# A convolution with group norm on one core: VectorE's and ScalarE's instruction queues aligned to a boundary of 128 instructions

## Chip, cores and metric

One core of a Trainium2 chip. The metric is the device time of one execution in microseconds; a kernel's time is the median of several runs. A profile is a separate record of one execution with every instruction and every DMA packet.

## What is computed

The input x has 8 images of 32 channels, 128 x 128, in float32. Group norm over 16 groups (two channels each) is followed by a 3 x 3 convolution done by FFT in the reference, and the result is added to x:

```
def _gn(v, G=16, eps=1e-5):
    g = v.reshape(B_, G, C_ // G, H_, W_)
    ...
    return ((g - m) / jnp.sqrt(s + eps)).reshape(v.shape)
...
    fout = jnp.einsum('bihw,oihw->bohw', fx, wf)
    sp = jnp.fft.ifft2(fout, norm='ortho').real
    ...
    out = sp[:, :, sh:sh + out_h, sw:sw + out_w]
    return out + bias[None, :, None, None]
...
x = x + _L0_conv_ref(_gn(x), L0_conv_weight, L0_conv_bias, 1, 1)
```

The reference pads to 256 x 256, multiplies the spectra, and cuts out a 128 x 128 window that begins 64 rows and columns in. Only the upper left part of that window holds convolution output; elsewhere the padding gives zero, so there the result is x plus the bias.

## The kernel before

**Layout.** The host splits each image into its four phases (even and odd rows and columns), so that the 32 channels times 4 phases fill 128 partitions, with 64 x 64 values of an image in each. Images lie in SBUF in pairs (`x0` to `x3`) and are updated in place. The weights and the bias come in one small array, `wb_sb`, and ScalarE spreads them into the 128 x 512 tile `w_sb` (line 181).

**Order of the work.** There is no scheduler. Every instruction is emitted through `Queues.__call__` (line 63), which puts it at the end of its engine's queue with the semaphore waits that it needs, so the order of the source is the order on each engine. `sp` issues all transfers: eight loads at the start (line 117, images 0 and 1 in halves, 2 and 3 whole, the rest in pairs, the weights after the first half) and seven stores (line 320: pairs 0 and 1 whole, images 4, 5 and 6 one by one, image 7 in two parts).

For an image, VectorE takes statistics in eight pieces (line 210) and joins them (221); ScalarE forms the terms (223, 226); TensorE averages over the group by the matrix `avg` (234); ScalarE and VectorE alternate over small columns to get scale and shift (243, 248, 252, 254, 257); ScalarE writes the normalised part needed into `g` (266) and adds the bias to the parts of x without convolution output (281). TensorE multiplies in three chunks of four float32 matmuls (297); VectorE adds product and bias to x (312), and the store follows. The statistics of image n + 2 and the normalising of image n + 1 run while TensorE multiplies image n.

**The top of the program.** After a barrier of all engines, GpSimd builds a mask (141 to 151), VectorE writes `eps` (152) and makes `avg` (155 to 163), and ScalarE loads its table and runs one activation on `warm` (166). Then ScalarE waits for the weights and VectorE for the first half of image 0.

**Instruction queues.** [...] The kernel's own part is some 115 instructions on ScalarE, 105 on VectorE and 437 on TensorE. [...]

## Time and profile before

| | before |
|---|---|
| median of 4 runs | 84.71 us (84.43, 84.48, 84.94, 85.06) |
| profiled execution's own time | 84.43 us |
| its span in the profile | 83.2 us |
| first load issued, first data packet | 0.79 us, 1.79 us |
| TensorE's last matmul ends | 73.4 us |
| last store issued | 74.93 us |
| HBM read, written | 16.82 MB, 16.78 MB |

In the lines of the profile, L297 is line 297 of the kernel; PE is TensorE's matmul, PEld its weight load, DVE is VectorE, ACT ScalarE, SPq the queue of SyncE that issues transfers. A row of digits shows the span in 40 equal slices, with the busy share of each in tenths. A line of DMA queues gives packets, MB, and the packets' time as a share of 16 DMA engines. A wait line reads: engine and line that waited, what released it, total us, times, longest us. A line that begins with a stretch such as 42.00:52.00 gives its length, then busy time and count of PE, PEld, DVE, ACT and POOL, the granted TensorE clock, the DMA share and GB/s.

### The profile page before, as it was taken

What the parts mean: (1) busy time and instruction counts of PE and PEld (TensorE: products, weight loads), DVE (VectorE), ACT (ScalarE), POOL (GpSimd) and SP (SyncE); (2) the same over time, 40 slices, a digit from 0 to 9 for tenths busy, and PEclk for the clock granted to TensorE, in tenths of its full rate; (3) what the DMA queues carried; (4) which work ended last, traced back from release to release, by engine and by line L of the source; (5) the groups of instructions that cost most, each with busy time, mean ns of one, the idle gap of its engine ahead of it and who ended that gap; (6) DMA issues with size and microseconds to landing.
All of it is one profiled execution on the core that took longest, in us unless ns stands there. A gap on an engine that the chain in (4) does not pass through costs nothing.

```text
span 83.2 us, 697 instructions
## 1 busy us (share of the span) xinstructions
PE 65.0 (78%) x214; PEld 39.4 (47%) x214; DVE 54.5 (66%) x103; ACT 51.8 (62%) x102; POOL 2.3 (3%) x8
## 2 busy tenths in 40 slices
PE   0000998999999999999999999999999999920000
PEld 0000531666666566656666666666566666600000
DVE  0339927982999799699969969996997250060000
ACT  6019437994995798499569958965994895000000
POOL 6400000000000000000000000000000000000000
PEclk9999999999999999999999999999999999996555
DMA  2899999999997999699989998999899999999991
GB/s 47 339 410 433 418 429 465 402 465 394 504 504 315 441 504 449 299 489 504 260 347 425 473 457 378 425 504 410 378 402 425 441 433 441 418 441 387 428 421 65
DMA packets 2211, 33.63 MB, mean 404 GB/s; under 512 B 256, under 2 KB 288, under 8 KB 416
## 3 DMA queue, kind: packets, MB, share of 16 engines
q1 hardware_dynamic: 2208, 33.60, 96.1%
q8 instruction: 1, 0.02, 0.1%
q14 instruction: 2, 0.02, 0.1%
HBM read 16.82 MB, written 16.78 MB: 404 GB/s over the span
## 4 chain that ended last, share of the span: by engine, by line
PE 76%; DMA 8%; DVE 2%; ACT 2%; SPq 1%; issue 1%
PE ps L297 70%; DMA x<-x_dram 8%; PE ps_w L330 5%; DVE x L312 2%; PE ps_m L234 1%; SPq L117 1%; ACT g L266 1%; ACT std L252 0%; ACT square L243 0%; ACT rstd L257 0%; DVE rstd L254 0%; DVE var L248 0%
## 5 line engine op out<-in xcount | busy, mean ns | idle before, releaser
L297 PE MATMUL ps<-g,w_sb 128*128 128x363 f32 (+1 forms) x192 | 59.0, 464 | 0.2 <-ACT g L266 0.2
L297 PEld LDWEIGHTS ps<-g,w_sb 128*128 128x128 f32 x192 | 35.2, 189 | 21.5 <-ACT g L266 2.0
L210 DVE BATCH_NORM_STATS2 stats<-x 128x6 f32<-128x512 f32 x64 | 38.7, 677 | 2.3 <-DMA x<-x_dram 2.2
L281 ACT ACTIVATE x<-x,bs_sb 128x1984 f32<-128x1984 f32 (+1 forms) x16 | 23.9, 1540 | 0.3
L312 DVE SCALAR_TENSOR_TENSOR x<-ps,bs_sb,x 128x1089 f32<-128x1089 f32 (+2 forms) x9 | 10.5, 1180 | 7.2 <-PE ps L297 7.2
L266 ACT ACTIVATE g<-x,rstd 128x396 f32<-128x396 f32 (+1 forms) x16 | 12.7, 838 | 0.3
L330 PE MATMUL ps_w<-x,avg 128*128 128x512 f32 x6 | 5.8, 1111 | 8.2 <-DMA x<-x_dram 8.2
L330 PEld LDWEIGHTS ps_w<-x,avg 128*128 128x128 f32 x6 | 1.7, 326 | 9.2 <-DMA x<-x_dram 8.2
L243 ACT ACTIVATE square<-ps_m 128x7 f32<-128x7 f32 x8 | 1.4, 176 | 5.7 <-PE ps_m L234 5.7
L223 ACT ACTIVATE terms<-bs_sb,mv 128x8 f32<-128x8 f32 x8 | 2.4, 302 | 3.6 <-DVE mv L221 3.6
L248 DVE COPY var<-ps_m 128x1 f32<-128x1 f32 x8 | 1.3, 158 | 5.1 <-ACT square L243 5.1
L234 PEld LDWEIGHTS ps_m<-terms,avg 128*128 128x128 f32 x16 | 3.2, 205 | 2.8 <-ACT terms L226 1.3
L252 ACT ACTIVATE std<-var 128x1 f32<-128x1 f32 x8 | 2.4, 295 | 1.8 <-DVE var L248 1.8
L257 ACT ACTIVATE rstd<-ps_m,rstd 128x1 f32<-128x1 f32 x8 | 2.1, 261 | 1.8 <-DVE rstd L254 1.8
L254 DVE RECIPROCAL rstd<-std 128x1 f32<-128x1 f32 x8 | 1.3, 164 | 2.9 <-ACT std L252 2.9
L221 DVE BATCH_NORM_AGGREGATE mv<-stats 128x2 f32<-128x48 f32 x8 | 3.0, 372 | 0.3
L181 ACT ACTIVATE bs_sb<-wb_sb 32x9 f32<-32x9 f32 x4 | 0.8, 210 | 3.7 <-DMA wb_sb<-wb_dram 3.6
L181 ACT ACTIVATE w_sb<-wb_sb 32x64 f32<-32x64 f32 (+2 forms) x16 | 2.8, 244 | 0.0
L234 PE MATMUL ps_m<-terms,avg 128*128 128x9 f32 x16 | 2.5, 230 | 0.0
L226 ACT ACTIVATE terms<-mv,eps 128x1 f32<-128x1 f32 x8 | 2.2, 279 | 0.0
L166 ACT ACT_TABLE_LOAD x1 | 1.3, 1283 | 0.8 <-PEq L411 0.8
L243 ACT ACTIVATION_READ_ACCUMULATOR square<-ps_m 128x1 f32 x8 | 1.6, 194 | 0.0
(12 smaller groups left out, 3.6 us busy)
## 6 DMA issues: line engine op xcount, KB each, us to landing
x<-x_dram SPq DMA_DIRECT2D x2, 4096.0 KB, 34.5
out_dram<-x SPq DMA_DIRECT2D x2, 4096.0 KB, 17.1
out_dram<-x SPq DMA_DIRECT2D x3, 2048.0 KB, 10.6
x<-x_dram SPq DMA_DIRECT2D x4, 1024.0 KB, 7.5
x<-x_dram SPq DMA_DIRECT2D x2, 2048.0 KB, 17.1
out_dram<-x SPq DMA_DIRECT2D x1, 1056.0 KB, 8.2
out_dram<-x SPq DMA_DIRECT2D x1, 992.0 KB, 11.8
wb_sb<-wb_dram SPq DMA_DIRECT2D x1, 40.5 KB, 4.6
```

The source lines that it names most:

```text
L181: return put("act", lambda e: e.activation(to, of, AF.Identity), weights_in, w_zero, mark=True)
L210: lambda e: e.bn_stats(stats[img][:, s, :], xts[img][:, STATS * s : STATS * (s + 1), :].rearrange("p h w -> p (h w)"),),
L221: "dve", lambda e: e.bn_aggr(mv, stats[img].rearrange("p n s -> p (n s)")), stats_ok[img], mark=True
L223: put("act", lambda e: e.activation(t[:, 0:NSIGN], signs, AF.Identity, scale=mv[:, 0:1]), mv_ok, bias_ok)
L234: lambda e: e.matmul(ps_ms[:, 0 : NSIGN + 1], avg, terms[img], start=True, stop=True),
L243: lambda e: e.activation(squares[img], ps_ms[:, 1:NSIGN], AF.Square, accum_out=var[:, 0:1]),
L252: "act", lambda e: e.activation(std, var[:, 0:1], AF.Sqrt, bias=var[:, 1:2]), square_ok, copied, mark=True
L266: lambda e: e.activation(g[:, rows, :], xt[:, LO + rows.start : LO + rows.stop, LO:W], AF.Identity, bias=rstd[:, 1:2], scale=rstd[:, 0:1],),
L281: put("act", lambda e: e.activation(part, part, AF.Identity, bias=bias_sb), *free, mark=True)
L297: lambda e: e.matmul(ps[:, 0:rows, 0 : N - dc], w_sb[:, k * P : (k + 1) * P], g[:, top : top + rows, dc:N], start=(k == 0), stop=(k == 3),),
L312: lambda e: e.scalar_tensor_tensor(part, in0=ps, scalar=bias_sb, in1=part, op0=ALU.add, op1=ALU.add),
L330: "pe", lambda e: e.matmul(ps_w, avg, piece, start=True, stop=True),
```

## The change

Behind the opening barrier, ahead of all other work of the kernel, VectorE and ScalarE get one directive each:

```diff
 NSIGN = 8
+PAGE = 128
 LANDED = 16
...
     put = Queues(nc)
+
+    for engine in (nc.vector, nc.scalar):
+        engine.addr_align(PAGE, offset=0, max_nops=0)
```

`addr_align` is not an instruction that computes. The loader reads it when it lays out the engine's final stream and places the next instruction at a multiple of 128 instruction slots[...]; the slots left over ahead of it are dead, and with `max_nops=0` one branch skips them. TensorE, GpSimd and SyncE get none. Nothing else changes: all instructions, waits and transfers are those of before, in the same order on every engine, four lines further down in the source.

## Prediction

> **What bounds the kernel now.** I read the page first: busy shares, the forty slices, the DMA queues, then the chain.

> ```profile
> PE 65.0 (78%) x214; PEld 39.4 (47%) x214; DVE 54.5 (66%) x103; ACT 51.8 (62%) x102; POOL 2.3 (3%) x8
> DMA  2899999999997999699989998999899999999991
> GB/s 47 339 410 433 418 429 465 402 465 394 504 504 315 441 504 449 299 489 504 260 347 425 473 457 378 425 504 410 378 402 425 441 433 441 418 441 387 428 421 65
> q1 hardware_dynamic: 2208, 33.60, 96.1%
> q8 instruction: 1, 0.02, 0.1%
> q14 instruction: 2, 0.02, 0.1%
> ```

> The compute engines are busy 62 to 78%, the data queue 96% of all 16 DMA engines' time. The last slice (81.1 to 83.2 us) holds 65 GB/s: most DMA engines have finished there, a few haven't. Three packets are labelled "instruction"; the change touches those.

> The chain says "PE ps L297 70%", which misleads: it follows releases, not queues. The DMA queue's own waits and a table of stages put this right.

> ```profile
> SPq L376 <- DMA out_dram<-x: 7.9, 1, 7.9
> ...
> 42.00:52.00 10.00, 10.00 (x37) 6.26 (x36) 8.86 (x18) 8.02 (x14) 0.00 (x0) 1.00 1.00 429
> ...
> 72.00:81.00 9.00, 1.39 (x5) 0.59 (x4) 1.48 (x2) 0.00 (x0) 0.00 (x0) 0.70 0.99 422
> 81.00:83.20 2.20, 0.00 (x0) 0.00 (x0) 0.00 (x0) 0.00 (x0) 0.00 (x0) 0.50 0.19 77
> ```

> The end waits 7.9 us for stores. The DMA share is 0.98 to 1.03 from 2 to 81 us, also after TensorE's last matmul (73.4 us). The last store is issued at 74.93 us, but by the packet records no DMA engine reaches its data before 78.4 us: 3.4 MB of older stores stand ahead. So 33.6 MB through 16 DMA engines set the end, and the latest of the 16 ends it.

> The packet records give each engine's finish: the 4-byte semaphore write by which every DMA engine closes each transfer. Microseconds behind the first engine, sorted:

> ```
> load ending 22.1 us: 0 .02 .05 .06 .17 .19 .19 .19 .21 .21 .22 .24 .25 .30 .32 .40
> load ending 42.1 us: 0 .07 .11 .12 .21 .36 .36 .37 .38 .41 .42 .57 .61 1.15 1.48 1.82
> last store, 81.0 us: 0 .07 .11 .12 .36 .36 .37 .38 .41 .43 .57 .61 .89 1.16 1.48 1.82
> ```

> Three engines fall far behind between 22 and 42 us, and since none is ever idle, none catches up. In that stretch lie the three instruction packets:

> ```profile
> DMA packets 29, 0.44 MB, mean 1106 GB/s; under 512 B 14, under 2 KB 14, under 8 KB 14
> q1 hardware_dynamic: 27, 0.43, 259.0%
> q14 instruction: 2, 0.02, 11.9%
> ```

> That is the DMA view of 31.8 to 32.2 us: both q14 packets. The one of q8 lies in 40.4 to 40.6 us. I joined each packet's end to the start next to it (all within 25 ns), which gives 16 unbroken rows from 30 to 46 us:

> - engine A: instruction packet at 31.815 us (8192 bytes, 0.333 us), then a data packet of 1.868 us where its like take 1.213; closes the load at 43.58 (the 1.48 above)
> - engine B: at 32.109 us (8192 bytes, 0.427 us), then a data packet of 1.672; closes at 43.92 (the 1.82)
> - engine C: at 40.486 us (q8, 16384 bytes, 1.016 us); closes at 43.25 (the 1.15)

> The three late engines are the three that carried an instruction packet.

> [...]

> **The change part by part.** Nothing is removed; no instruction of the computation changes its order or queue on any engine. ACT and DVE get one directive each, behind the opening barrier and ahead of their first instruction. The loader turns it into one jump over unused slots.

> 1. *The jump.* [...] From A's 0.333 us and SP's 1.0 us from issue (0.79) to first packet (1.79) I estimate at most 1.4 us. Both are covered:

> ```profile
> ACT bs_sb L181 <- DMA wb_sb<-wb_dram: 3.6, 1, 3.6
> DVE stats L210 <- DMA x<-x_dram: 2.2, 1, 2.2
> DVE avg L155 <- POOL pair L145: 1.7, 1, 1.7
> ```

> ACT may start 3.6 us later before the weight spreading (5.87 us) moves; DVE 1.7 us before its first addition moves and some 3.8 us before the statistics (5.60 us) do. The instructions queued behind the jump (table load, warm-up; eps, the averaging matrix) all lie in that cover. Without it, 1.5 us more are free: the tightest store (image 5, issued at 63.84) is reached by the DMA engines at 66.3 and needs 1.0 to start. SP and POOL get no directive. Cost 0.

> 2. *The two q14 fetches.* I take them to be ACT's and DVE's crossing into their next block: ACT is near its row 60 of 115, DVE near row 50 of 105[...]. After the jump each body begins at a block's first slot. ACT's body is 113 instructions and DVE's 103, both under 128, so neither crosses again before its last instruction. Crossings and their fetches move from 32 us to 0.8 us. The data packets begin at 1.79 us, so a fetch of 0.33 to 0.43 us fits ahead if it starts by 1.35; one that waits the full 1.0 us of SP's start touches the first load.

> 3. *The end.* Without their fetches A and B should close with the other thirteen (0 to 0.89). C keeps its own: 1.157. End gain: 1.821 - 1.157 = 0.664 us. The two packets alone would be worth less; the slowed data packets behind them (0.655 and 0.459) go too.

> Sum against the profiled execution (84.43 us, span 83.2): span 82.5, time 83.77. The median of the four runs is 0.28 above that execution, so 84.71 - 0.66 = 84.05 us. Bounds of this step: no gain if the fetches still meet data at full price; 1.821 - 0.889 = 0.93 us if C gets lighter too (its packet runs amid slow packets on all engines around 41 us, so it may vary).

> **Rivals.**

> *The fetch lands in the first load* (partial). For: 0.8 plus 1.0 is 1.8 us. Against: the first data packets are staggered over 1.79 to 2.45 us anyway. A lag of 0.4 to 0.6 plus 0.33 stays below C, full gain; plus the full 0.99 (0.333 + 0.655) gives 1.4 to 1.6, gain 0.2 to 0.4: 84.4 us.

> *The change doesn't do what it says.* The fetch may not be tied to the block's edge where I think, or what the runtime runs after the body crosses a block (ACT's body ends some 15 slots short of it) and fetches at 70 us under the stores. Then the late engine is only another: 84.6 to 84.8 us.

> *Slower: the jump throws the fetched blocks away.* ACT and DVE each fetch two blocks afresh at the top, under the first load. Two at A's price are 2 x 0.99 = 1.98 us on one DMA engine, never made up: 0.4 to 0.6 plus 1.98 against 1.82 is 0.6 to 0.8 us slower, 85.3 to 85.5. It decides once over 1.2 us is added to one engine (1.82 - 0.61). Against: at 32 us the next block was evidently there, as neither engine stopped.

> *No fetch matters.* DMA bytes are equal and 8 KB is 0.02% of them, which speaks for no change; the table of finishes speaks against it.

> **How the numbers follow.** Fetches clear of the data: 0.58, 84.05 us, own range 83.6 to 84.4. Partial: 0.14, 84.4. No effect: 0.19, 84.7. Slower by refetch: 0.09, 85.4. About 1% (0.85 us) is what a measurement of this kernel can tell from no change. The four runs spread 84.43 to 85.06; if the high ones are a worse day of A or B, the main case gains more than 0.66. So 0.31 of faster by over 1% comes from the main case (half of it), 0.64 within 1%, and 0.05 slower by over 1% from the refetch with a third block. The range 83.5 to 85.0 leaves out the refetch and the far end of the main case.

> **What would show it.** In the changed kernel no q14 packet at 10 to 75 us; two before 2 us; one q8 packet near 40 us still; one late DMA engine (C) instead of three, so the last slice emptier; busy times of all engines as before, TensorE's last matmul at 73.4 within 0.2 us. Wrong if two engines still close 1.4 us or more behind, if q14 packets appear near 70 us, or if ACT's or DVE's first instruction moves by over 3 us.

## The result and the profile after

No change that can be measured: the median is 84.80 us after (84.06 to 86.25) and 84.67 us for the kernel before, run beside it (84.06 to 86.45). The ratio is 1.0011, 95% interval 0.9995 to 1.0027. Forecast was 84.05 us. The profiled execution after took 84.8 us (span 83.6); that of before had taken 84.43. The medians here count all executions, the ratios leave out those over 1.5% above the fastest of the same kernel.

The page after, same rows as before:

```profile
PE 65.0 (78%) x214; PEld 39.4 (47%) x214; DVE 54.6 (65%) x103; ACT 51.8 (62%) x102; POOL 2.3 (3%) x8
DMA  2899999999999899799898999999899999999991
q1 hardware_dynamic: 2208, 33.60, 95.6%
q14 instruction: 2, 0.02, 0.1%
q8 instruction: 1, 0.02, 0.1%
```

The same work, the same full DMA engines, the same three instruction packets. They did move. The DMA view of the kernel after, first for 1.8 to 3.6 us, then its row for 31.8 to 32.2 us, where both q14 packets lay before:

```profile
q1 hardware_dynamic: 63, 0.52, 89.6%
q14 instruction: 2, 0.02, 6.0%
```

```profile
q1 hardware_dynamic: 24, 0.43, 248.5%
```

So the fetches (the instruction packets of q14, called ScalarE's and VectorE's from the runs with one directive alone, below) left the middle and came to the top, but not ahead of the data. By the packet records they start at 1.828 and 3.344 us, and the first data packet at 1.812. They also take longer there: 0.958 and 0.760 us, against 0.333 and 0.427 before.

The timeline at the top of the kernel after (start, duration, engine) shows the jump:

```profile
0.80 0.38 SPq L121 DMA_DIRECT2D x<-x_dram  x1
...
1.23 1.28 ACT L170 ACT_TABLE_LOAD   x1 [1.23 <-PEq L415]
...
1.42 0.06 DVE L156 MEMSET eps<- 128x1 f32 x1 [1.42 <-PEq L415]
```

The table load stands 0.45 us later than before (0.78), `eps` 0.56 us later (0.86). The trace has the jump itself as a branch at 0.786 us on ScalarE (0.033 us) and at 0.818 on VectorE (0.047 us); the rest, 0.41 and 0.55 us, is a stall behind it. Both lie in the cover that the prediction named. ScalarE's wait for the weights is 3.9 us after (3.6 before), so the jump reached nothing.

The first loads themselves end later. TensorE waits for the second half of image 0; after, then before:

```profile
PE ps_w L334 <- DMA x<-x_dram: 9.1, 1, 9.1
```

```profile
PE ps_w L330 <- DMA x<-x_dram: 8.2, 1, 8.2
```

All that hangs on TensorE moves with it: its last matmul ends at 74.3 us (73.4 before) and the last store is issued at 75.86 (74.93). The DMA engines reach that store's data at 78.46 us, as before (78.43), so this doesn't set the end.

How far the 16 DMA engines are behind the first one, from the semaphore writes in the packet records, as in the prediction (us). The first row is the sixth load of x; further down, "the third transfer" is the second half of image 0, which the first engine ends at 7.3 to 7.9 us (9.6 where the loads are held):

```
load ending 22.1 us: 0 .05 .09 .10 .15 .17 .18 .19 .20 .22 .29 .38 .42 1.07 1.26 1.29
load ending 42.1 us: 0 .01 .09 .14 .23 .24 .35 .46 .46 .48 .58 .62 1.44 1.66 2.08 2.17
last store, 81.0 us: 0 .09 .14 .23 .24 .35 .46 .46 .48 .58 .62 .74 1.66 1.84 2.08 2.17
```

Before, all 16 were within 0.40 us at 22 us. Now three are late there already, one more than there are fetches, and the latest ends 2.17 us behind instead of 1.82. Stages show the same tail. Before:

```profile
81.00:82.00 1.00, 0.00 (x0) 0.00 (x0) 0.00 (x0) 0.00 (x0) 0.00 (x0) 0.50 0.35 144
82.00:83.00 1.00, 0.00 (x0) 0.00 (x0) 0.00 (x0) 0.00 (x0) 0.00 (x0) 0.50 0.06 25
```

After:

```profile
81.00:82.00 1.00, 0.00 (x0) 0.00 (x0) 0.00 (x0) 0.00 (x0) 0.00 (x0) 0.50 0.40 169
82.00:83.00 1.00, 0.00 (x0) 0.00 (x0) 0.00 (x0) 0.00 (x0) 0.00 (x0) 0.50 0.20 84
```

The next to last number is the DMA share; one engine alone is 0.06. From 82 us on there is about one engine's work left before, three engines' after.

### The profile page after: what moved, and what is told of

The parts are those of the page before. It is cut to its first block, busy times and chain, and to the rows that moved or that the text cites. A ratio compares the mean times of both kernels' runs of the same rounds, so it can differ in the third digit from the quotient of the medians.

```text
span 83.6 us, 699 instructions
## 1 busy us (share of the span) xinstructions
PE 65.0 (78%) x214; PEld 39.4 (47%) x214; DVE 54.6 (65%) x103; ACT 51.8 (62%) x102; POOL 2.3 (3%) x8
## 3 DMA queue, kind: packets, MB, share of 16 engines
q1 hardware_dynamic: 2208, 33.60, 95.6%
## 4 chain that ended last, share of the span: by engine, by line
PE 76%; DMA 9%; DVE 2%; ACT 2%; SPq 1%; issue 1%
PE ps L301 70%; DMA x<-x_dram 9%; PE ps_w L334 5%; DVE x L316 2%; PE ps_m L238 1%; SPq L121 1%; ACT g L270 1%; ACT std L256 0%; ACT square L247 0%; ACT rstd L261 0%; DVE rstd L258 0%; DVE var L252 0%
## 6 DMA issues: line engine op xcount, KB each, us to landing
wb_sb<-wb_dram SPq DMA_DIRECT2D x1, 40.5 KB, 5.4
```

## Experiments

The theory: a fetch costs the DMA engine that carries it up to 1 us wherever it meets data, no engine catches up, and the latest engine ends the kernel. The rival: the fetches are too small to matter and the late engines have another cause. In every profile here the execution's time is 1.64 to 1.70 us more than the last engine's last semaphore write (84.43 - 82.77 before, 84.80 - 83.15 after, 86.61 - 84.91 in the slowest below). That the latest engine sets the time is thereby given; the question is what makes it late.

**Directives ahead of the barrier** (twice, then with TensorE, for which `(nc.tensor, 2 * PAGE)` is added to the loop). The jumps are put in front of the opening barrier, 0.7 us earlier:

```diff
-    for engine in (nc.vector, nc.scalar):
-        engine.addr_align(PAGE, offset=0, max_nops=0)
+    block = nc.m.functions[0].blocks[0]
+    ahead = list(block.instructions)
+    for engine, page in ((nc.vector, PAGE), (nc.scalar, PAGE)):
+        engine.addr_align(page, offset=0, max_nops=0)
+    every = list(block.instructions)
+    for align in every[len(ahead):]:
+        at = next(n for n, i in enumerate(ahead) if i.engine == align.engine)
+        ahead.insert(at, align)
+    block.instructions = ahead
```

> The two directives stand ahead of the opening barrier instead of behind it, so the jumps come some 0.7 us earlier. Theory (a fetch costs its DMA engine about 1 us wherever it meets data, and the latest of the 16 engines ends the kernel): the q14 packets start at about 1.1 us, 1.04 us after the jump as in the changed kernel, and are over before the first data packet at 1.8 us; only the engine of TensorE's fetch (q8) stays late, the spread of the 16 engines at the end falls from 2.17 us to about 1.2, and the end comes 0.5 to 0.7 us earlier than before (ratio 0.992 to 0.995), less up to 0.2 us by which the barrier may open later. Rival (the lateness of some DMA engines isn't the fetches' doing): the spread stays near 2 us and the ratio is 1.000 or above.

Ratio 0.9986 (0.9963 to 1.0010), medians 84.66 and 84.66 us. The DMA view of 1.1 to 1.9 us, all packets that there are:

```profile
DMA packets 2, 0.02 MB, mean 20 GB/s; under 512 B 0, under 2 KB 0, under 8 KB 0
## 3 DMA queue, kind: packets, MB, share of 16 engines
q14 instruction: 2, 0.02, 5.1%
```

The fetches (1.331 and 1.485 us, 0.324 us each) are clear of the data, which start at 1.953, 0.16 us late. Yet the gain isn't there. In this execution engines are up to 1.32 us late at the third transfer, without a fetch among the data, and the q8 engine is last, 1.76 us behind. So the fetches are out of the data, as the theory said, and the gain that it promised isn't there.

> The run with the two directives ahead of the barrier, once more, for a second profile and a narrower interval. If its 10 us of engine time lost at 5 to 6 us was an accident of one execution, the second profile doesn't have it, the spread at the end is about 1.2 us, and the ratio goes below 0.997. If the early fetches cause it, it is there again and the ratio stays at 0.997 to 1.001.

Ratio 0.9992 (0.9965 to 1.0018). The first profile had lost 10 us of DMA engine time at 5 to 6 us, in slow packets and idle engines; that was an accident (2 us here), but two engines are again 1.16 and 1.38 us late at the third transfer. One of them is the last of all (1.96 us behind at the end), the q8 engine the next (1.79).

> As the run with the two directives ahead of the barrier, and TensorE gets one too, at a boundary of 256 instructions (its fetch is 16384 bytes). Theory: no instruction packet lies in the data stretch if TensorE's 437 instructions cross only one more block edge near its row 256; if the q8 fetch is tied to that second edge, one stays, but later or earlier than 40 us. With none left the spread at the end is 0.6 to 0.9 us and the end 0.9 to 1.2 us earlier than before (ratio 0.986 to 0.990); with one left as in the other run, 0.992 to 0.995. Rival: spread and time as before, 1.000.

Ratio 1.0027 (1.0003 to 1.0050). The page shows what the third directive did:

```profile
q8 instruction: 2, 0.03, 0.2%
q14 instruction: 2, 0.02, 0.1%
```

TensorE fetches at 1.361 us and again at 48.979; what brings the second fetch isn't shown. So its fetch in the middle is moved (from 40.486 us before), not removed, and SyncE's second issue takes 1.456 us instead of 0.415.

**One engine at a time.** `for engine in (nc.vector,)` and `(nc.scalar,)` in the change's loop.

> Only VectorE is aligned (behind the barrier, as in the change). Theory: one q14 packet near 1.8 to 3.4 us, which is VectorE's, and one near 32 us, which is ScalarE's; two DMA engines are late by about 1 us for them and a third for q8, so the time is that of before, ratio 0.995 to 1.005. Rival (the jump itself, or ScalarE's directive, makes the early lag): no engine over 0.5 us late at 22 us.

Ratio 1.0025 (1.0002 to 1.0048). q14 packets at 3.165 us (0.800 us long) and at 31.825.

> Only ScalarE is aligned. Theory: the mirror of the run with VectorE alone: one q14 packet early (ScalarE's), one near 32 us (VectorE's), three late DMA engines at the end, ratio 0.995 to 1.005. Rival: no engine over 0.5 us late at 22 us.

Ratio 1.0041 (1.0017 to 1.0064). q14 packets at 1.815 us (1.119 us long) and at 32.083. So ScalarE's fetch starts 1.0 us after its jump and VectorE's 2.3 us after; the attribution in the prediction holds. With VectorE alone one engine is 1.18 us late at 22 us. With ScalarE alone two are, by 0.61 and 0.76.

**The jump without a fetch at the top:** `offset=100` in the change.

> The change with offset 100 instead of 0: the bodies begin at slot 100 of the block in which they are already, if they stood before at slot 60 to 90 as I work out from the place of the fetches. The jump is then there without a fetch at the top, and both engines cross into the next block some 28 instructions later. Theory: no q14 packet before 10 us, two at 15 to 22 us (the crossing and about 4 us in the DMA engine's queue), time as before, ratio 0.997 to 1.003. Rival (the jump itself disturbs the first loads): late engines at 8 us and long issues by SyncE though no fetch is there.

Ratio 1.0019 (0.9989 to 1.0049). The DMA view of 12 to 15.2 us:

```profile
q1 hardware_dynamic: 111, 1.42, 106.2%
q14 instruction: 2, 0.02, 1.3%
```

The packets are at 12.206 and 14.818 us, earlier than the 15 to 22 that I expected. Up to the third transfer all engines are within 0.38 us, so in this profile the jump alone makes none late. At 22 us two engines are late by 0.77 and 1.21: each fetch has taken its price, there as at 32 us. One ends 2.14 us behind.

**More fetches.** The kernel before with directives in the middle; in `for img in range(B)`:

```diff
+        if img in (4, 5, 6):
+            nc.vector.addr_align(128, offset=0, max_nops=0)
```

> The kernel before with three more directives on VectorE alone, for images 4, 5 and 6 (about 42, 49 and 57 us): three more q14 packets on one DMA engine. Theory: that engine falls 2.4 to 3 us further behind and the end comes 2.4 to 3 us later less its distance to the latest (0 to 0.4): ratio 1.025 to 1.035. Rival: ratio 0.998 to 1.004. The stall after each jump (0.4 to 0.55 us as at the top of the changed kernel) is VectorE's and has over 1.5 us of cover before the stores.

Ratio 1.0231 (1.0189 to 1.0273), 86.66 against 84.60 us: 24 KB more on one DMA engine cost 2 us. Its page and its last stages:

```profile
q14 instruction: 5, 0.04, 0.1%
```

```profile
81.00:82.00 1.00, 0.00 (x0) 0.00 (x0) 0.00 (x0) 0.00 (x0) 0.00 (x0) 0.50 0.36 151
82.00:83.00 1.00, 0.00 (x0) 0.00 (x0) 0.00 (x0) 0.00 (x0) 0.00 (x0) 0.50 0.12 50
83.00:84.00 1.00, 0.00 (x0) 0.00 (x0) 0.00 (x0) 0.00 (x0) 0.00 (x0) 0.50 0.08 34
84.00:85.30 1.30, 0.00 (x0) 0.00 (x0) 0.00 (x0) 0.00 (x0) 0.00 (x0) 0.50 0.03 13
```

From 83 us on a single engine works; it closes 3.90 us behind the first, the next at 1.71. The rows of packets put the three added fetches, and VectorE's own at 33.2 us, on this one engine. This settles that a fetch among the data costs its engine some 0.7 us (2.06 us of the kernel's time over three) and that one late engine sets the end. The rival is refuted. One step of the expectation failed: no stall of 0.4 us follows these jumps; the statistics go on 0.05 us behind them.

> The kernel before with one directive each for VectorE and ScalarE in the middle (when image 5's products begin, about 50 us): it adds one q14 packet for each engine under the stores. Theory: if each lands on the DMA engine that already carried that engine's fetch, those two engines lose another 0.8 to 1.0 us and the end comes 0.8 to 1.0 us later (ratio 1.009 to 1.012). Rival (fetches don't set the end): ratio 0.998 to 1.003; 16 KB more is 0.05% of the bytes.

The edit is the same with `if img == 5` and both engines. Ratio 1.0058 (1.0034 to 1.0083), 0.5 us: the right sign, about half the size. The profile caught an execution of 85.92 us, far above the median of 85.07; there the latest engine (3.09 us behind) is not one that got an added fetch.

**The fetches in a quiet place.** The loads wait until GpSimd has zeroed `w_sb`, in the kernel before and in the changed one; the lines that issue them stand behind that memset:

```diff
-        return put("sp", lambda sp: sp.dma_start(to, of), adds=name)
+        return put("sp", lambda sp: sp.dma_start(to, of), w_zero, adds=name)
```

> The kernel before, with its loads held until GpSimd has zeroed the weight tile (about 3.0 us in the trace), so data start about 2.3 us later. It is the base for the next run: q14 packets near 34 us, three DMA engines late at the end by 1.1 to 1.9 us, time 2.0 to 2.4 us above before (ratio 1.024 to 1.028) under every theory.

> The changed kernel with the same hold of its loads. The q14 packets (1.1 to 1.5 us after the jumps) are over before the data begin at about 4.1 us. Theory (a fetch costs about 1 us on its DMA engine if it meets data and nothing if it doesn't; the latest engine ends the kernel): no engine over 0.5 us late at the end of the sixth load, only the q8 engine late at the end, and the time is 0.5 to 0.8 us below the run with the kernel before held (ratio between the two 0.991 to 0.994). Rival (removing the fetches from the data brings nothing, since something else makes the late engines or the end): equal to the held kernel before within 0.2 us.

86.93 and 86.61 us, ratios 1.0257 (1.0218 to 1.0296) and 1.0237 (1.0185 to 1.0289) to before. The difference of 0.2 to 0.3 us has the expected sign, but the intervals cover each other: not decided. In the profiles it is as expected: the held changed kernel's fetches (2.0 us) are over before its data (4.07), its engines are within 0.31 us at the sixth load, and only q8's is late at the end, by 1.21, against 1.85 us in the held kernel before. But by its row of packets the engine that is 1.85 us behind there is q8's too, so the two profiles don't show what clearing the q14 fetches is worth.

**The last two loads issued later.** In six profiles SyncE's issue of the last load took 0.85 to 1.0 us instead of 0.46 and some engine was late from then on. To take that away, the loads of pairs 2 and 3 wait for the weights (`load` gets a parameter for this):

```diff
-        loaded[2 * pair] = loaded[2 * pair + 1] = [(H, load(pairs[pair], x[pair]))]
+        loaded[2 * pair] = loaded[2 * pair + 1] = [(H, load(pairs[pair], x[pair], weights_in))]
```

> The kernel before, with the last two loads (pairs 2 and 3) issued only when the weights have landed (5.8 us; the DMA engines reach their data at 22 us). Theory [...]: no engine late by over 0.5 us at the third transfer, late engines at the end only from the fetches (1.1 to 1.9 us): ratio 0.995 to 0.999. Rival (the early lateness has nothing to do with the last issue): as before, 1.000.

Ratio 1.0001 (0.9977 to 1.0025).

> The late-issue kernel before, a second profile: q14 fetches at 32 us again, with two engines late by 1.3 to 1.9 us at the end. No engine late by over 0.5 us at the third transfer if the late issue has taken the starved engine away.

In the first profile all engines are within 0.45 us at the third transfer; in this one an engine is 1.36 us late there, although no issue took over 0.50 us. The slow issue is therefore not the cause of it.

> The same late issue with the two directives ahead of the barrier. Theory: neither a starved engine nor a q14 fetch among the data, only the q8 engine late at the end (1.2 us): ratio 0.989 to 0.994, that is 0.5 to 0.7 us below the late-issue kernel before. Rival (early fetches disturb the first loads by themselves): engines late by 1 us at the third transfer and a ratio of 0.997 to 1.001.

Ratio 1.0005 (0.9979 to 1.0031).

> The same late issue in the changed kernel. Theory: its fetches still meet the first load (packets of 0.7 to 1.1 us), two engines late by about 1 us: as the late-issue kernel before, ratio 0.995 to 1.001. If it lies at 0.993 or below, the changed kernel's loss was the starved engine too.

Ratio 1.0041 (1.0020 to 1.0061), q14 packets at 1.821 and 3.319 us.

> The late issue with the directives ahead of the barrier, a second profile. If lateness from the first loads makes the slow executions: a time above 84.5 us comes with an engine late by over 0.9 us at the sixth load, a time near 84.0 with none. If not: a time above 84.5 with a small spread and a late mean of the 16 engines.

> A third profile of the same kernel; as for the second: the spread at the sixth load and at the end go with the time (about 84.0 us at 1.1 us of spread, 0.5 to 1 us more with a spread of 1.6 to 2.1), or the mean of the engines does.

Three executions of one kernel, the late issue with the directives ahead of the barrier, took 83.99, 85.24 and 85.02 us. The first and the second one's last stages:

```profile
81.00:82.00 1.00, 0.00 (x0) 0.00 (x0) 0.00 (x0) 0.00 (x0) 0.00 (x0) 0.50 0.43 177
82.00:83.00 1.00, 0.00 (x0) 0.00 (x0) 0.00 (x0) 0.00 (x0) 0.00 (x0) 0.50 0.02 8
```

```profile
81.00:82.00 1.00, 0.00 (x0) 0.00 (x0) 0.00 (x0) 0.00 (x0) 0.00 (x0) 0.50 0.72 304
82.00:83.00 1.00, 0.00 (x0) 0.00 (x0) 0.00 (x0) 0.00 (x0) 0.00 (x0) 0.50 0.08 34
83.00:84.00 1.00, 0.00 (x0) 0.00 (x0) 0.00 (x0) 0.00 (x0) 0.00 (x0) 0.50 0.02 8
```

The first is the picture that the prediction drew: no engine late by over 1 us but the q8 engine, by 1.09, and the end 0.44 us before that of the profile of before. In the other two the q8 engine is last as well, but 2.25 us behind, and the mean of the 16 is 0.2 to 0.3 us later. The price of TensorE's fetch is not a constant. The two slower executions also have an engine late by 1.05 and 1.12 us at the sixth load (0.43 in the fast one), which had been expected of them.

**The profiles again.** Unchanged kernels:

> The kernel before, unchanged, for a second profile. If an engine late by over 1 us at the third transfer comes and goes by execution (two kernels that equal the one before up to 42 us had one, the first profile of the kernel before had none), this profile may have either; three late engines from the fetches at 32 and 40 us are there in any case.

85.22 us. The fetches are at 33.1, 33.3 and 42.5 us, and an engine without any of them is 1.64 us late at the third transfer. It is last at the end, by 2.53 us; the q8 engine is next with 1.68.

> The changed kernel once more, for a second profile: q14 packets again at 1.8 to 3.5 us, at over twice the 0.31 us of such a packet elsewhere, and two or three engines late by 0.9 to 1.3 us at the sixth load.

84.54 us. The fetches are at 1.876 us (0.938 us long) and 3.361 (0.713), three engines are 1.13 to 1.33 us late at the sixth load; the last ends 1.89 us behind, the q8 engine 1.83.

**Empty engines in the first loads.** The packet records say more than the finishes. In eight of the 20 profiles 16 packets are under way at all times from 4.8 us to the end of the third transfer. In the other twelve there are fewer for a while, between 4.8 and 6.2 us (7.2 to 8.0 in the held kernel before): one or more DMA engines stand empty behind the packets of the weights, for 0.3 to over 1 us. The 8 KB packet that comes next often takes about 1.0 us instead of 0.31. In the second profile of before, the late engine stops at 5.07 us and goes on at 5.61 with a packet of 1.02 us. In all twelve profiles an engine is 1.05 to 1.64 us late at the third transfer. In the eight none is by over 0.45 us, except with a fetch among the first data (VectorE alone 1.17, ScalarE alone 0.74, the change with late issue 1.08).

Both profiles of the changed kernel are among the twelve. By the rows of packets, two of the three late engines in the first one stood empty (between 4.79 and 6.16 us); one is late by its fetch, that of 3.344 us. Empty engines occur with and without directives: in five of the seven profiles with none at the top, in seven of the ten with both at offset 0, in none of the other three (one engine alone, offset 100). But summed over the engines they last 0.9 to 2.1 us with both, and 0.2 to 0.8 without where loads aren't held. Whether early jumps and fetches lengthen them was not tested; it would be another reason why the directives ahead of the barrier gain nothing.

**The q8 engine.** Where the q8 fetch starts and how far its engine ends behind the first, in 14 profiles:

```
kernel                         q8 fetch starts, us   its engine at the end, us behind
before                             40.5                  1.16
offset 100                         40.4                  1.20
ScalarE alone                      40.5                  1.12
late issue, before                 40.3                  1.28
late issue, ahead                  40.7                  1.09
late issue, ahead (2nd, 3rd)       41.9, 41.4            2.25, 2.25
late issue, before (2nd)           42.6                  1.83
late issue, after                  42.6                  1.81
before (2nd)                       42.5                  1.68
after, both                        42.6, 42.7            1.84, 1.83
ahead, both                        42.6, 42.8            1.76, 1.79
```

## Why the prediction was wrong, point by point

*What bounds the kernel:* right. DMA engines set the end, the latest of them in particular: three added fetches moved the end by 2 us, and TensorE's 0.9 us of delay in the changed kernel moved nothing. One figure was misread: when the last store is issued, 1.6 MB of older stores stand ahead by the packet records, not 3.4.

*Step 1, the jump:* right in effect. It costs 0.45 and 0.56 us at the top, under the 1.4 us estimated and in the cover named. The branch itself (COMPARE_BRANCH in the trace) has records of 0.033 and 0.047 us, and the statistics go on 0.05 us behind a jump in the middle. At the top a stall comes on top of it, and as it ends at 1.23 and 1.42 us, before the q14 packets start (1.828 and 3.344), it isn't a wait for them; what it waits for isn't shown. The slower rival, in which each jump brings two blocks afresh, was a guess, and it did not occur: two q14 packets, not four.

*Step 2, the fetches ahead of the data:* wrong. "So a fetch of 0.33 to 0.43 us fits ahead if it starts by 1.35"; they start at 1.83 and 3.34. I had both ends of this (1.0 us from SP's start lands on 1.8 us), put 0.58 on the good end and 0.14 on the other. And the partial rival was priced too low: among the first loads a fetch takes 0.7 to 1.1 us (once 0.31) instead of 0.33 to 0.43. Where no engine stood empty, engines at 22 us are late by 1.18 (VectorE alone), 0.61 and 0.76 (ScalarE alone), and 0.67 and 1.07 us (both, late issue). What A and B saved at 32 us was in good part paid at 2 us. That a fetch belongs to a block's edge was the prediction's assumption; what the runs show is that the packets move with the directives, from 32 us to 1.8 and 3.3 with offset 0 and to 12.2 and 14.8 with offset 100.

*Step 3, "C keeps its own: 1.157":* wrong, and this would have spoiled the forecast even with step 2 right. The gain was the difference of two numbers of one execution, B's 1.82 and C's 1.157. The table shows that 1.157 was at the low end: the q8 engine ends 1.1 to 1.3 us behind where its fetch starts near 40.5 us, 1.7 to 1.8 where it starts at 42.5 to 42.8, and 2.25 in between, about the time when the engines turn from loads to stores. In nine of its 14 profiles it is 1.68 or more, about as large as B's 1.82, so taking A and B away leaves the maximum where it is. A second contributor I had not seen at all: in the second profile of before, an engine without a fetch is 1.64 us late from the first loads on and ends last. That "none is ever idle" held for the first profile of before only. The runs with the fetches clear of the data agree with this (0.9986 and 0.9992, where I expected 0.992 to 0.995, and 1.0005 with the late issue).

*The signs and the range.* As forecast, no q14 packet lies between 10 and 75 us, one q8 packet stays (42.6 us), and the busy times are those of before. But the second fetch starts at 3.34 us instead of before 2, TensorE's last matmul ends at 74.3 us instead of 73.4, and four engines close 1.66 us or more behind instead of one. That 84.80 us lies in the range of 83.5 to 85.0 is luck as far as the main case goes (83.6 to 84.4). The rival that gave 84.6 to 84.8 us had the late engine as "only another", which fits, but by fetches that stay or come at 70 us, which doesn't.

*What stays open:* why DMA engines stand empty at 5 us in some executions and not in others, and why the q8 fetch starts now near 40.5 and now near 42.6 us. My guess of the slow last issue fell. The held pair leaves it undecided whether clearing the fetches brings some 0.2 us. No version here is measurably faster than the kernel before.

## What to carry to other kernels

Here all DMA engines were full of data from 2 to 81 us (share 0.98 to 1.03 before), and the time was the latest engine's: in every profile it was 1.64 to 1.70 us more than that engine's last semaphore write. Each engine's semaphore writes show who is late and since when. A small packet on one engine counted in full: three fetches of 8 KB cost 2.06 us, some 0.7 us each. But a gain worked out by taking one late engine out of one profile is not to be trusted: it is a maximum over several engines whose lateness varied by a microsecond between executions (the q8 engine's from 1.09 to 2.25 us), so look at a second profile before pricing it.

## What the runs showed of the hardware that was not expected

The instruction fetches came much later where the DMA engines were full of data. In the kernel with three added directives, with q1 at 100.2% of the 16 engines' time from 47 to 62.6 us, the jumps are at 43.37, 50.75 and 58.13 us and the packets start at 47.47, 55.39 and 62.22, that is 4.1 to 4.6 us later; with no data about, the packets started 1.0 to 1.4 us after the jump (at 1.331 and 1.485 us with the directives ahead of the barrier). VectorE didn't wait for the late ones: it went on 0.05 us after each jump.

Data packets behind a fetch were slow too: 1.868 and 1.672 us before, against 1.213. And around the turn from loads to stores, at 40 to 42 us, 17 packets of 32 KB on the 16 engines took 1.5 to 2.2 us in the profile of before, against the same 1.213.
